# A two-layer block with experts on one core: phase sums with heads on partitions, part of the rounding on GpSimd, the shared expert moved to the logits, and a new order table

## The chip, the cores and the metric

The kernel runs on 1 core of a Trainium2 chip. The metric is the device time of the whole kernel in microseconds (us), taken as the median of three runs. A separate profiled execution gives the trace; its own time is stated beside the runs below.

## The reference, cut to what matters

The input x has 16 sequences of 512 tokens with 128 channels. Four stages follow one another, each with a residual sum and a layernorm:

```python
x = layernorm(x + L0_attn(x))   # 16 heads of 64: cumulative sums along the sequence, with gates
x = layernorm(x + L0_ffn(x))    # 8 experts, one per token (argmax), relu
x = layernorm(x + L1_attn(x))   # 16 heads of 8: softmax attention with a table of position biases
x = layernorm(x + L1_ffn(x))    # one shared expert for all tokens + 8 routed ones (argmax), swiglu
```

Two parts of it are touched by the change. In the first attention, two phases are added to the scores; they depend on the position n and not on the data:

```python
n  = linspace(0, 1, 512)
p1 = sum(sin(a1 * n + b1) * c, axis=-2)      # a1, b1, c: (16 heads, 64, 1) -> (16, 512)
p2 = sum(sin(a2 * n + b2) * c, axis=-2)
```

In the last stage the shared expert is `shared_out = (silu(x @ wg.T) * (x @ wu.T)) @ wd.T`, where x is the output of the third stage's layernorm; the routed experts' output and the residual are added to it. The routing logits are `x @ gate_w.T` of the same x.

## The kernel before

**The program as a list of operations.** The kernel does not issue instructions as it goes through its loops. Each step is handed to a planner with `op(engine, cost, emit, reads, writes)` (L215): an engine, an estimated cost in us, a function that emits the instructions, and the tiles read and written. When all 6210 operations are known, `order()` (L243) fixes one sequence of all of them. It takes, on each engine that its clockwork shows as free, the operation with the lowest rank whose inputs are there and whose buffers can be had. The ranks come from the table `ORDER` (L52): two characters per operation, in the order in which the operations were declared; with DIGITS (91 characters) their place is 91 times the first index plus the second. The places in the table are a permutation, that is a complete order. At the end (L1751 and below) the chain of operations is emitted in this order, so each engine's queue, SP's queue of transfers and GpSimd's queue among them, is fixed when the program is built. An engine works its queue strictly from the front.

**Buffers.** Tiles come from pools by kind (`kinds`, L331): among them six of `w2` (128 x 1024 floats), five of `p`, four of `ld`, three of `mid`, two of `xt` (128 x 512), eight of `x`, which hold the sequences, and in PSUM three of `pair` and two of `one`.

**The head.** `phases` (L471) makes the sines. The 16 x 64 = 1024 sine rows of a phase lie on 128 partitions in 8 groups; a "quarter" is two groups in one `w2` tile `arg`. For each quarter: VectorE makes one angle row (`first`, L478), ScalarE the other (`second`, L484); ScalarE divides by 2 pi and rounds with two activations (`whole`, L491 and L494); VectorE takes whole turns off with two scalar_tensor_tensor instructions and clips (`reduced`, L499 and L502); ScalarE takes the sine (L511). When all four quarters of a phase are there, `sums` (L517 to L524) multiplies on TensorE: for each of 4 token blocks, 8 matmuls with a 128 x 128 block of sines as the stationary operand and `cblk` with 16 columns as the moving one, so that tokens come out on partitions and heads along the free axis. The result is copied to `p1`, or clipped and exponentiated to `p2e`. Many first loads carry `p1` as a gate: the list of tokens to be cleared (`lists`, L693), the experts' table (`table`, L544), `ow`, `wr`, `br` and `rev` are issued on SP behind it. `slide` (L568) builds the position bias: a line per head goes to DRAM, 16 transfers `slid<-line` (L627) bring 128 shifted copies back, and TensorE reverses each (`turn_ps`, L636).

**The two attentions.** `attention0` (L971) computes scores, gates and then four token tiles per sequence (`tile0`, L1038): values `pv` (L1048), their product with the scores `ev` (L1061), GpSimd's product `self` (L1067), the carry of the tile before added by a transfer from GpSimd's queue (L1074), the prefix product `cum` (L1083) and the way out through `po` and `y`. `attention1` (L1210) goes over 4 groups of 4 heads and 4 token tiles: a rounded pass for the maxima (`s`, L1286 and L1293, `low`, `tops`), then scores `st` (L1359), bias sum on VectorE (L1374), exponential on ScalarE (L1380), product `av` (L1389).

**The experts.** Sequences go in chunks of 2, 3, 4, 4, 2 and 1. For each chunk tokens are routed (`route`, L721), scattered to a list in DRAM sorted by expert (`scatter`, L839), fetched four slots of 128 tokens at a time (`slots`, L891), multiplied with the weights of the slot's expert, which GpSimd fetches by index, and gathered back (`gather`, L869). In the last stage, `mixture1` (L1483), the chunk's tokens are scaled and scattered, and then, for each sequence of the chunk, comes the shared expert: the sequence is transposed once more (`transposed`, L682: four TensorE transposes and a ScalarE copy, L687 and L690, tiles `pt_m` and `xt_m`), multiplied with `wgs` and `wus` (L1519), joined by `swiglu`, multiplied with `wds` (L1528), added to x in place (L1536) and stored to `out` (L1543). The slots follow. At the end `out` is read back, the routed part is added, and the last layernorm is applied.

`second` (L1652) runs `attention1`, a layernorm and `logits` (L1595) for each sequence of a chunk. `logits` makes a transposed copy `xt` of the same x.

Of the kernel before, what the change touches and what calls it, by code (L numbers as in the profile page):

```python
# [52 lines left out]
    "###$#P#8#N#R#H#1#6#<#B#Q#.#0#4#>#L#?#3#A#J#W#@#/#F#U#[#_#i#O#9#T#]#a#Y#Z#^#b#c#d#e#h#q#v#g#k#o#u"  # L53
    "#|$$$*$,#)#&#*#l#~$##z#y#n#}#p#I#V#`#G#E#%#,#-#S#(#M#D#X#m#s$/$2$5#w$&$;$+$1$8$@$D$G$I$K#t$-$A$F"
    "$J$N$O$P$X$]$b$e$H$T$Y$^$f$j$k$o$v$z%3%7$_$d$g$m${$~%#%&%*%-%2%8%>%@%E%I%L%O#r#K#'$i$n$p$t$y$|$}"
    "%%%(%)%.%/%0%6%:%<%A%1%4%5%;%B%F%G%J%N%P%R%V%?%C%D%K%U%X%Y%]%`%b%h%k%Q%S%T%Z%c%f%g%j%n%t%z%|&%&)"
    "&,&-&.&0&1&2&8&=&D&U&3&6&;&a&:&l&p&t&y'#')',&b'-&|'$'@'C'F'J'L&r'M'O'T'`'f'j'n'o'''p'q'u(&(+(2(5"
    "(7(=(N(Q(Z(^(O(_(e(l(t#:#2#5#7#;#C#f#j$r%$%'$E$U$Z#{$%$.$)$:$>$B$M$R$L$[$`$a$l$s$3$=$C$S$q$w$'$6"
    "$9$($7$<#x$0$4$?$Q$V$x%H%M$u%9%=$W$c$h&$%v%y#=(a(c(m(y(f(r(u(k(p(x)#(s(w)$).({):)l)o)b)k){)])a)-"
    ")3)m)5);)9)?)I)@)C)0)7)O*)*/*1)+)6)')2)%)8)/)4*J*M*R*Q*U*Y)B)F)D)J)T*o*t*x*s*u*z)H)M)K)P)Z*y*|*~"  # L60
    "*}+$+,)W)^)Q)V)d+#+*+/+&+++2)_)g)U)Y)w)}*#*'+5+9+@)p)q)i)j+'+-+)+(*T*[*_*W*Z*h*L*P*:*A*S*f*i*l*j"
    "*q*v*8*<*4*9*C+0+3+8+6+:+D*+*0)~***6+7+B+H+;+A+L*>*D*%*-*G*`*d+4+Q+V+Z)e)c)X)[+C+>+?+<+G+N+T+S+X"
    "+b)z*&*2*5*;+Y+_+a+`+d+h)u)y)r)v*(+e+k+p+g+m+{*B*F*]*a*e+x+|,$+~,',+)x)|)n)t*,+J+M+O,/,4,7+n+r+v"
    "+q+s,@,(,,,1,0,3,J,5,:,>,F,M,`,E,L,S,R,W,c,f,{-#-7-C-I-R-U-Y-g-j-n.,.4+},%-]-d,.,<,6,;,8,V,T,=,D"
    ",A,C,Q,K,r,w,x,~-(-+-0,a,d-9,p,s,X,_,y,k,o-3-<-D-T-^-a,H,I,?,Y,[,O,N,U-l-p-t-s-w-},v,z,|-'-1-x.#"
    ".+.&.-.0,],b,g,j,m.*.1.6...2.;-$-,---5-?.7.<.C.B.F.R,i,l,n,q,u-G-N-P.W.^.b-2-/-8-;.:.@.?.=.D.H.L"
    ".K.S.c-E-J-~.%.).T.[.a.Y.].h-@-F-X-`-i._.i.m.f.j.y-V-Z-M-S-b.k.s.x.o.t/(-c-h-_-f-m.9.>.J/+/2/8-)"
    "-*-6-4.u.p.q.r.v.z.}.|/$/*-:->-B-H-L/%/)/-/,///5-=-A-Q-W-[/7/;/>/</@/D.'./-u-|.5/A/E/I/H/L/R-o-r"
    "-K-O-y.P.V.~/V/`/c/./1/6/4/9/G/J/N/Q/P/T/[/U/X/Z/Y/b/h/a/g/j/i/m/q/v/x/|00070C0T0`0f0k0v0x0~1&%+"
    "%,%W%[%^%_%a%d%e%i%l%m%q%r%s%x%~&&&+%p%u%{&(&/&4&5&9&>&A&G&L&#&'&*&7&<&?&@&C&J&N&S&W&B&F&O&R&X&["  # L70
    "&^&`&c&i&m&o&s&v'('+'.'1%o%w%}&E&H&I&K&M&Q&P&T&]&V&Y&Z&_&g&j&x&{&d&h&k&q&z&}&~'&'*'/'8'>&n&u&w'%"
    "'4':';'?'B'E'['a'0'3'6'='D'G'H'K'P'W']'b'e'h'w'z'|(#&e&f'2'5'7'9'<'A'I'N'X'U'Y'Z'_'d'i't'x'R'V'^"
    "'c'm'r's'v'y'}(-(3'g'k'l'{(*(.(/(1(6(:(;(@'~(%(((0(9(<(>(A(C(J(U(V(](d(j(o(q(z(})()1)A)L)f*$)&))"
    ")G*=)=*H*K*b*g+R+W+[*?+]+f+i+t+y,9,B,^*N,G,t,}-e-k-q-v-z+l-{.$.(.G.N.X.`.d-%.e.g.l.{/&/:/?/B/O/l"
    "/p/t/z/f0%0*010@/y090G0O0Y151<1A1O1=1@1F1[1C1q1W1_1x2)1{2'20282;2>1H1P2,2:21272@2r2w2x2*1K22252Q"
    "2]2V2Z2a3,33362&323T3V3f4%3k3n404L4P4S264Q5$5(5w695}6&6@787=7B3Y:j6b6i;#;&;';);+;/;3;5;A;`;h;i;m"
    ";s;x;S;j;w;|;~<)<,#+/~0$050=0&0-020.0/06080A030D0Q0J0:0M0V0X0^0d0o0u0w1#1(0_0h0S0Z0s0I0P0[0a0n12"
    "171:0>0U0R0N0H0?0B0K1u1w1z1y2#2%0y1'0q0z1,1}2+2.2$2(2/0c0m0l0p0{24292<2=2A2K1+111)1-1;2B2D2I2H2P"
    "2U0g0j1.191J1S1X1]2Y2c2f0t0r0}0|2F2G2E2J2O2T2^2W2[2p1G1M1D1I1U2e2j2o2i2k2y181>1N1Y1g2l2s2u2q2t3)"
    "141B1?1E1^2v2z3$3#3&311$1*1L1R1b1o1t2S35393?101/16132{2|3%2~3'3*3.3-303O1V1e1`1c1j343;3A383=3U1Q"  # L80
    "1T1l1p1|3H3K3L3R3X3d1d1h1f1k1s3Q3[3_3W3]3j1r1v1Z1a2-2?2b3+3m4#4)3a3g3i3h3p443r3w3}3|4(494/474=45"
    "484A5?5C5I5G5L5T5Y5d5i5l5o5r5y5~6%64676;6?6C3^3e3l3q3o3s3t3y3v4-4*4.3~433z3x3{4O4T4>4E4W4J4M4F4I"
    "4N4m4q4R4V4x4i4n4U4Z4s5,51534$4,4&415F5H5B5D5J5N5P5O5U5p4v4|4_4c5&5V5]5_5^5b6'4D4G4b4g4l5j5u5{5s"
    "5v60464:4<4?4C6#6*6/6.62654H4K4]4`4d595>5Q686A6D4r4p4Y4[6(6,6-6)63666<6:6>6H4}5%4o4u5/6E6I6L6K6O"
    "6Z5'5*4t4w556S6W6]6a6f6j50565-525<6g6v6{6r6x7+575:5m5q5z6U6Y6[70717>4{4z4f4h6o6k6p6m757:7A797;7F"
    "6J6N6_6c6h7<7C7J7@7D7M6|7#6q6u7-7I7K7P7O7T7W6P6T6X6`6e7U7Y7^7]7c7y7/736d6l7H7L7N7Q8#8+827e7k7r7p"
    "7w7}7s8$8*7z8&8-8'8,808.838881858>8;8@8C8G8K8N8O8W8`8h8m8r8y9+9/929F7X7[7_7f7a7l7n7j7g7m7o7~7q8%"
    "7u7x7t8R8e8A8D8i8=8J8M8T8^8V8Z8?8B8d8E8P848:8U8n8s8w7{7|8)8(8789868<9-969A91989E90938p8v9:9C9G9L"
    "9J9P9V8H8L8c8g8q9K9O9R9Q9U9_8j8z8[8a9#9S9]9d9b9f9j9&9*8l8o9.9H9I9M9p9t9v8Y8]8S8Q9Y9[9a9W9e9h9m9k"
    "9y9~8}9'9)9,9>9z9}:&:#:-:9979;999=9B:0:8:=:5:;:@9<9@9g9i9n:>:G:J:B:H:V9l9q9o9s9x9|:%:':[:`:e9594"  # L90
    "8x8u:C:F:D:A:X:_:f:Z:b:r:$:)9r9w:,:g:l:n:m:q:w:(:+:.:1:<:o:u:z:s:v;,:6:?:I:M:Q:y:|:~:};%;8:O:S:L"
    ":P:U:Y:^:a;=;L;O;2;:;?;7;<;N;>;C;E;D;H;P;F;K;R;Q;U;X;V;Z;_;];c;e;g;k;n;p;r;u;}<%<*<-</<0<1<2'S'Q"
    "($('()(,(4(8(?(B(G(H(L(M(P(R(S(W([(D(I(K(Y(b(g(h(n(v(~)N)S(T(X(`(i(|),)*)<*E*I*O*X*.*3*7*@*V*^*c"
    "*k*m+o+u+w+z,&,e,h-&-.(F(E)>)E)R)`)h)s*r*w*{+=+E+F+K+P+U,P,Z+%+.+1+I,#,*,),2.3.8.n.w+^+c+j,-.M.Z"
    ".Q.U/0/3/e/o/=/C/F/K/k/s/w0#0'0;0E0L0W0]0b0e0i1%*p*n.A.E.I.O/#/'/M/S/]/W/^/_/d/n/r/{0)0,040<0F1i"
    "1m1n232X2_2h2n/u/}0+1~2C2M2N2R373:3B3I2`2d2g2m2}3(3/3>3F3u4'4+424;4@4B4e4k0(2L3<3@3E3G3M3P3J3N3S"
    "3Z3b3`3c5)5.5A5K4X4^4a4j4y4~5#5+5;5@5[5c54585=5E5`5e5f5n5t5x5|6$5M5S5X5h6+616=6B6F6M6Q6R6V6^6n6s"
    "6t6y6z6~7'72777R7h8/7%7(7d8F7E8X8_8f8k8t8|9$8I9%8{8~9?9D9N9T9^8b9X9Z9`9u9{:*:/:29(:3:4:7:R:W:c:h"
    ":k9c;4:t:x;J;M;T;W;Y::;a;[;b;q;v;{<#<&<.<B<E<I<P<?<R<V<c<n<X<r<z=g=n='=H>(>->2<3<4<8<=<5<6<9<O<<"
    "<j<7=L<><A<C<G<H<J<N<a<k<o<K<M<Q<S<U<Z<]<i<x<~<:<;<@<L<D<F<T<Y<_<`=j=<=w=}>/>=>6>9>B>F>J>N=i>K>I"  # L100
    ">M>y?6?#?.?;?R?Y?Z>$?X?L?OB#C$B)B/C+C4C;C=>QC:CGCQC}DlD'D*DtESEYE]?SI2F.F9IJIMIOIQIRITI[I_IgJ4J;"
    "JCJKJPJTJ>NwO%O-O7OCOML&O)O?ONOQOlOp<W<[<q<w<^<g<e<b<d<l<y<f<h=0=/=2<m=B=F=8=A=K=1=7<v<}=?=-=4=$"
    "=+=9=U=X<|=&=u>'>.>1=#=*<u<s<{=%=,<t>V>[>_>^>b>e=E=I=J=O=[>`>d>g>f>j>o=G=M=6=:=R>t>z>}>w>{?-=W=_"
    "=N=T=d>~?%?+?*?/?3=]=b=@=C=k=q=x={?7?:?>=Z=Y=>==?'?&?,?)?0?5?9?8?<?A=m=p=z>#>,???B?G?E?I?N=t=y>+"
# [101 lines left out]
class Plan:  # L206
# [8 lines left out]
    def op(self, engine, cost, emit, reads=(), writes=(), delay=None):  # L215
        if delay is None:
            delay = (0.25, 0.12, 0.15, 0.15, 3.4)[engine]
# [104 lines left out]
def block_kernel(ctx: ExitStack, tc: tile.TileContext, d, out: bass.AP):  # L322
# [144 lines left out]
    def col(t):  # L467
        return slice(t * P, (t + 1) * P)
# [1390 lines left out]
```

## Time and profile before

| what | us |
|---|---|
| median of 3 runs | 2387.21 |
| lowest and highest run | 2380.75, 2396.14 |
| profiled execution, its own time | 2306.71 |
| span of the profile (first to last instruction) | 2305.0 |
| TensorE busy in the span | 2123.2 |
| VectorE busy | 1805.3 |
| ScalarE busy | 1468.9 |
| GpSimd busy | 759.6 |

The profile is of one execution, which was shorter than the three timed runs. Lines of the profile name the engine (PE is TensorE's matmuls, PEld its weight loads, DVE VectorE, ACT ScalarE, POOL GpSimd, SPq the issuing of transfers on SyncE), the source line, the operation and the tiles, written as output<-input with buffer numbers left out. A group has "busy, mean ns of one" and, behind the next bar, the idle time of the engine just ahead of it and what ended it. One fp32 matmul of the program shows as two records on PE. Times of a timeline are in us from the span's start: start, length, and for the engine that waited, in brackets, how long and for what.

### The profile page before, as it was taken

Reading aid. Unit: us, or ns where it says so; the run is one execution under the profiler, and the core shown is the slowest. Engines: PE = TensorE matmul, PEld = TensorE weight load, DVE = VectorE, ACT = ScalarE, POOL = GpSimd, SP = SyncE. Lnnn points to the kernel's source line nnn. Section 1 sums busy time; section 2 is a strip of 40 time slices with the busy share of each in tenths; the row PEclk is TensorE's granted clock in tenths of the full one; section 3 lists DMA queues with packets and bytes.
Section 4 is the critical chain, followed back from the end, with each engine's and each line's share of the span. In section 5 each row is a group of like instructions: output and inputs, shape, how many; then the busy total and the mean of one; then the engine's idle time right before and its main releaser. Section 6 shows DMA issues by size and latency. Waiting matters only on the chain. (4 is left out here: it accounts for less than half of the span.)

```text
span 2305.0 us, 34824 instructions
## 1 busy us (share of the span) xinstructions
PE 2123.2 (92%) x12723; PEld 1086.2 (47%) x12820; DVE 1805.3 (78%) x3286; ACT 1468.9 (64%) x1848; POOL 759.6 (33%) x763
## 2 busy tenths in 40 slices
PE   5898989999999998999999998999999999998994
PEld 4465744444545445454443443455534334544353
DVE  6355698788879787888878687988887999687973
ACT  6322367866576784667567876557687876676651
POOL 1134552134121425621214234422231424223524
PEclk9898999999999998999999998999999999999997
DMA  6522321211210333320102331212232211432334
GB/s 178 158 91 71 92 70 42 69 45 49 77 45 11 85 111 93 97 87 10 41 14 67 105 105 28 74 52 79 73 86 71 68 38 56 135 116 74 111 106 145
DMA packets 152446, 180.03 MB, mean 78 GB/s; under 512 B 19332, under 2 KB 125444, under 8 KB 152276
## 3 DMA queue, kind: packets, MB, share of 16 engines
q1 hardware_dynamic: 125588, 84.27, 13.7%
q0 software_dynamic: 26688, 93.53, 13.7%
q8 instruction: 101, 1.65, 0.3%
q14 instruction: 69, 0.57, 0.1%
HBM read 127.67 MB, written 42.93 MB: 74 GB/s over the span
## 5 line engine op out<-in xcount | busy, mean ns | idle before, releaser
L1380 ACT ACTIVATE p<-p 128x1024 f32<-128x1024 f32 x512 | 537.4, 1058 | 237.1 <-DVE p L1374 222.3
L1374 DVE TENSOR_TENSOR p<-st,bias 128x1024 f32<-128x1024 f32 x512 | 604.3, 1217 | 90.4 <-PE st L1359 80.3
L1308 ACT CAST low<-s 128x1024 bf16<-128x1024 f32 x512 | 495.0, 1020 | 113.6 <-PE s L1293 91.1
L823 POOL DMA_INDIRECT ws<-tab,rows x212 | 215.7, 1017 | 460.4 <-PE py L962 168.0
L1316 DVE TENSOR_TENSOR low<-low 128x1024 bf16<-128x1024 bf16 (+1 forms) x512 | 299.5, 585 | 78.7 <-ACT low L1308 69.8
L1359 PE MATMUL st<-qk_pad 32*128 32x512 f32 x2048 | 319.5, 646 | 3.9 <-DVE p L1374 3.6
L1286 PE MATMUL s<-bias,ident 128*128 128x512 bf16 x927 | 301.6, 398 | 10.3 <-ACT low L1308 3.2
L1389 PE MATMUL av<-p,vaug 128*32 128x512 f32 x2048 | 282.3, 609 | 7.6 <-ACT p L1380 6.2
L1067 POOL TENSOR_TENSOR self<-ev,own 128x1024 f32<-128x1024 f32 x64 | 125.3, 1957 | 429.1 <-DVE ev L1061 309.6
L1293 PE MATMUL s<-qk_pad 32*128 32x512 bf16 x1024 | 204.2, 391 | 24.0 <-issue 14.7
L1317 DVE TENSOR_REDUCE tops<-low 128x4 f32<-128x512 bf16 x256 | 175.5, 686 | 10.4
L1293 PEld LDWEIGHTS <-qk_pad 32*128 32x128 bf16 x1024 | 48.9, 91 | 244.0 <-issue 227.5
L823 POOL DMA_INDIRECT yg<-results,place x128 | 128.3, 1002 | 95.3 <-issue 38.3
L1359 PEld LDWEIGHTS st<-qk_pad 32*128 32x128 f32 x2048 | 93.6, 184 | 128.6 <-DVE p L1374 44.8
L1286 PEld LDWEIGHTS <-ident 128*128 128x128 bf16 x1024 | 75.1, 100 | 145.8 <-issue 142.7
L1083 PE MATMUL cum<-ev,tri 128*128 128x512 f32 x256 | 132.0, 640 | 10.5 <-DMA ev<-carry 8.6
L1114 PEld LDWEIGHTS y<-ow,ot 128*128 128x128 f32 x1024 | 122.7, 194 | 32.1 <-issue 19.2
L1114 PE MATMUL y<-ow,ot 128*128 128x128 f32 x1024 | 130.0, 281 | 2.1 <-DVE cnt L808 1.3
L1048 PE MATMUL pv<-vw,xt 128*128 128x512 f32 x256 | 128.1, 625 | 0.0
L962 PE MATMUL py<-ws,h 128*128 128x128 f32 x848 | 111.2, 285 | 9.3 <-DVE h L1478 5.2
L1061 DVE TENSOR_TENSOR ev<-pv,ex 128x1024 f32<-128x1024 f32 x64 | 78.0, 1219 | 52.8 <-PE pv L1048 25.9
L962 PEld LDWEIGHTS py<-ws,h 128*128 128x128 f32 x848 | 102.1, 196 | 36.7 <-issue 14.5
(191 smaller groups left out, 2903.4 us busy)
## 6 DMA issues: line engine op xcount, KB each, us to landing
xq<-tokens SPq DMA_DIRECT2D x44, 256.0 KB
results<-yq SPq DMA_DIRECT2D x44, 256.0 KB
qk_pad<-qk SPq DMA_DIRECT2D x256, 32.0 KB
slid<-line SPq DMA_DIRECT2D x16, 448.0 KB
tokens<-zero SPq DMA_DIRECT2D x4, 1472.0 KB
x<-in_x SPq DMA_DIRECT2D x16, 256.0 KB
xt<-in_xt SPq DMA_DIRECT2D x16, 256.0 KB
qk_pad<-qk SPq DMA_DIRECT2D x256, 16.0 KB
```

Source lines behind the costliest of these rows:

```text
L823: nc.gpsimd.indirect_dma_start(out, bass.IndirectOffsetOnAxis(to, 0) if to is not None else None, in_, bass.IndirectOffsetOnAxis(of, 0) if ...
L962: nc.tensor.matmul(py()[:, col(s)], h()[:, c, col(s)], ws[s]()[:, off + c * W : off + (c + 1) * W], start=(c == 0), stop=(c == 1),)
L1114: nc.tensor.matmul(y()[:, :P], ot()[:, hf, col(c)], ow[:, 4 * hf + c, :], start=(hf == 0 and c == 0), stop=(hf == 1 and c == 3),)
L1286: nc.tensor.matmul(s()[:, i, :], ident16, bias16[:, 4 * g + 2 * jp + i, 2 * u + 1 : 2 * (u + N) : 2], start=True, stop=False,)
L1293: nc.tensor.matmul(s()[:, i, :], pad[r, 0, col(it)], pad[r, 1, :], start=False, stop=True,)
L1308: lambda s=s, jp=jp, part=part: nc.scalar.copy(part(0, N)[:, 2 * jp : 2 * jp + 2, :], s()),
L1316: nc.vector.tensor_tensor(part(0, n), part(0, n), part(n, 2 * n), ALU.max)
L1317: nc.vector.tensor_reduce(tops[g % 2][:, it, :], part(0, N // 4), AX.X, ALU.max, negate=True)
L1359: nc.tensor.matmul(s[jp]()[:, i, :], pad[r, 1, col(jt)], pad[r, 0, :], start=True, stop=True,)
L1374: lambda jp=jp, h=h, pj=pj: nc.vector.tensor_tensor(pj(), s[jp](), bias[:, h : h + 2, u : u + N], ALU.add),
L1380: ACT, 1.0, lambda pj=pj: nc.scalar.activation(pj(), pj(), AF.Exp),
L1389: nc.tensor.matmul(acc()[32 * j : 32 * j + 32, :], va[:, jt, h * VW : h * VW + 32], p[j // 2]()[:, j % 2, :], start=(jt == 0), stop=(jt == ...
```

## The change

- **Phases.** Each quarter's sines are now the moving operand and `cblk` (16 columns) the stationary one: two matmuls of 512 columns per quarter, as soon as that quarter is done, accumulate heads on 16 partitions. ScalarE copies the sum (in a `us` tile), and four transposes bring tokens back on partitions.
- **Rounding.** In the odd quarters `whole` becomes two tensor_scalar instructions on GpSimd; in the even ones it stays on ScalarE.
- **Shared expert.** A new function `shared` holds what stood in `mixture1`. It is called in `second` right behind `logits`, for each sequence, and uses the transposed copy that `logits` made; the extra transposition goes. Its sum goes to a new `mid` tile `kept`, not to x, and is stored from there.
- **Costs.** The planner's default hand-over delays and some of its costs are changed (a stretch of such edits that hold no other change is left out below: `pv` and `cum` 1.72 to 1.8, `low` 1.03 to 0.93 and the like).
- **Order table.** All of `ORDER` is new. It has 6188 places in place of 6210 (10 operations more in the phases, 32 fewer in the transpositions), again a permutation. Read out, SP's queue begins with `lin`, `ab` and the clearing of two token lists; four `slid` transfers (heads 14, 13, 0, 15) stand ahead of the clearing of a third list and of the experts' table, the fifth (head 9) behind them; on TensorE the turns of these five heads stand ahead of the first `cum`, that of head 9 ahead of the gates' sums; VectorE copies `p1` behind the last `reduced`; the loading of `kone` comes later. In the last chunk the shared expert's first matmul stands ahead of `rank`.

```diff
 ORDER = (
-    "###$#P#8#N#R#H#1#6#<#B#Q#.#0#4#>#L#?#3#A#J#W#@#/#F#U#[#_#i#O#9#T#]#a#Y#Z#^#b#c#d#e#h#q#v#g#k#o#u"
...
+    "###$#J#>#9#F#;#'#)#,#2#=#*#-#/#<#M#1#0#6#H#S#P#(#Q#b#g#K#U#^#m#q#w#z#4#+#C#Z#a#A#.#D#T#]#_#h#k#o"
...
 )
@@ -214,7 +213,7 @@
 
     def op(self, engine, cost, emit, reads=(), writes=(), delay=None):
         if delay is None:
-            delay = (0.25, 0.12, 0.15, 0.15, 3.4)[engine]
+            delay = (0.13, 0.11, 0.12, 0.1, 3.4)[engine]
         o = Op(len(self.ops), self.due, engine, cost, delay, emit)
         self.ops.append(o)
         before = set()
@@ -505,26 +504,43 @@
 
                 op(ACT, 0.6, second, reads=["ab", lin], writes=[(arg, 1)])
                 op(DVE, 0.53, first, reads=["ab", lin], writes=[(arg, 0)])
-                op(ACT, 1.9, whole, reads=[(arg, 0), (arg, 1)], writes=[turns])
+                def whole_too(arg=arg, turns=turns):
+                    nc.gpsimd.tensor_scalar(turns(), arg(), INV2PI, ROUND, ALU.mult, ALU.add)
+                    nc.gpsimd.tensor_scalar(turns(), turns(), ROUND, None, ALU.subtract)
+
+                if quarter % 2:
+                    op(POOL, 4.0, whole_too, reads=[(arg, 0), (arg, 1)], writes=[turns])
+                else:
+                    op(ACT, 2.3, whole, reads=[(arg, 0), (arg, 1)], writes=[turns])
                 op(DVE, 3.2, reduced, reads=[turns], writes=[arg])
                 op(
-                    ACT, 1.0, lambda arg=arg: nc.scalar.activation(arg(), arg(), AF.Sin),
+                    ACT, 1.1, lambda arg=arg: nc.scalar.activation(arg(), arg(), AF.Sin),
                     writes=[arg],
                 )
                 sines.append(arg)
-            acc = buf("one", f"phase{which}")
-
-            def sums(acc=acc, sines=sines):
+            acc, sums = buf("one", f"phase{which}"), buf("us", f"sums{which}")
+            for quarter, sines_of in enumerate(sines):
+
+                def add(acc=acc, arg=sines_of, quarter=quarter):
+                    for j in (2 * quarter, 2 * quarter + 1):
+                        nc.tensor.matmul(
+                            acc()[:H0], cblk[:, j, :], arg()[:, j % 2, :], start=(j == 0),
+                            stop=(j == 7),
+                        )
+
+                op(PE, 3.0, add, reads=[sines_of, "cblk"], writes=[acc])
+            op(
+                ACT, 0.6, lambda acc=acc, sums=sums: nc.scalar.copy(sums()[:H0], acc()[:H0]),
+                reads=[acc], writes=[sums],
+            )
+
+            def turn(acc=acc, sums=sums):
                 for t in range(NT):
-                    for j in range(8):
-                        nc.tensor.matmul(
-                            acc()[:, t * H0 : (t + 1) * H0],
-                            sines[j // 2]()[:, j % 2, t * P : (t + 1) * P],
-                            cblk[:, j, :],
-                            start=(j == 0), stop=(j == 7),
-                        )
-
-            op(PE, 8.0, sums, reads=[*sines, "cblk"], writes=[acc])
+                    nc.tensor.transpose(
+                        acc()[:, t * H0 : (t + 1) * H0], sums()[:H0, col(t)], ident[:H0, :H0]
+                    )
+
+            op(PE, 0.6, turn, reads=[sums], writes=[acc])
 
             def av(acc=acc):
                 return acc()[:, : NT * H0].rearrange("p (t h) -> p t h", h=H0)
@@ -659,7 +675,7 @@
             for t in range(NT):
                 nc.vector.bn_aggr(mv()[:, t, :], st()[:, t, :])
 
-        op(DVE, 1.3, stats, reads=[x, *xs_of(x)], writes=[st, mv])
+        op(DVE, 1.08, stats, reads=[x, *xs_of(x)], writes=[st, mv])
 
         def scale():
             nc.gpsimd.tensor_scalar(rs(), mv()[:, :, 1], EPS, None, ALU.add)
...
@@ -1480,6 +1496,41 @@
         )
         return h
 
+    def shared(b, x, xt):
+
+
+        pg, pu = buf("pair", f"pg_s{b}"), buf("pair", f"pu_s{b}")
+        for w, ph, key in ((wg, pg, "wgs"), (wu, pu, "wus")):
+
+            def up(w=w, ph=ph):
+                for f in range(2):
+                    nc.tensor.matmul(ph()[:, f, :], w[:, col(f)], xt(), start=True, stop=True)
+
+            op(PE, 1.82, up, reads=[xt, key], writes=[ph])
+        h = swiglu(pg, pu, NT, f"s{b}")
+        py, kept = buf("one", f"py_s{b}"), buf("mid", f"kept_{b}")
+
+        def products():
+            for t in range(NT):
+                for f in range(2):
+                    nc.tensor.matmul(
+                        py()[:, col(t)], h()[:, f, col(t)], wd[:, f, :],
+                        start=(f == 0), stop=(f == 1),
+                    )
+
+        op(PE, 1.89, products, reads=[h, "wds"], writes=[py])
+        op(
+            DVE, 0.65,
+            lambda: nc.vector.scalar_tensor_tensor(
+                kept(), py(), 0.5, x(), ALU.mult, ALU.add
+            ),
+            reads=[py, x, *xs_of(x)], writes=[kept],
+        )
+        op(
+            SP, 0.45, lambda: nc.sync.dma_start(xout[b], tok(kept())), reads=[kept],
+            writes=[("out", b)],
+        )
+
     def mixture1(c, b0, xs, lg, store, span):
         n = f"m1_{c}"
         nt = CHUNKS[c] * NT
@@ -1508,42 +1559,6 @@
                 reads=[x, m], writes=[scaled, ("scaled", c, i)],
             )
             scatter(1, c, i, scaled, place, store)
-        for i, x in enumerate(xs):
-            plan.due = span(0.1 + 0.2 * i / len(xs))
-            xt = transposed(x, f"{n}_{i}", [("scaled", c, i)])
-            pg, pu = buf("pair", f"pg_{n}_{i}"), buf("pair", f"pu_{n}_{i}")
-            for w, ph, key in ((wg, pg, "wg"), (wu, pu, "wu")):
-
-                def up(w=w, ph=ph, xt=xt):
-                    for f in range(2):
-                        nc.tensor.matmul(ph()[:, f, :], w[:, col(f)], xt(), start=True, stop=True)
-
-                op(PE, 1.82, up, reads=[xt, key + "s"], writes=[ph])
-            h = swiglu(pg, pu, NT, f"{n}_{i}")
-            py = buf("one", f"pys_{n}_{i}")
-
-            def products(py=py, h=h):
-                for t in range(NT):
-                    for f in range(2):
-                        nc.tensor.matmul(
-                            py()[:, col(t)], h()[:, f, col(t)], wd[:, f, :],
-                            start=(f == 0), stop=(f == 1),
-                        )
-
-            op(PE, 1.89, products, reads=[h, "wds"], writes=[py])
-            op(
-                DVE, 0.65,
-                lambda x=x, py=py: nc.vector.scalar_tensor_tensor(
-                    x(), py(), 0.5, x(), ALU.mult, ALU.add
-                ),
-                reads=[py], writes=[x, *xs_of(x)],
-            )
-
-            op(
-                SP, 0.45, lambda i=i, x=x: nc.sync.dma_start(xout[b0 + i], tok(x())),
-                reads=[x], writes=[("out", b0 + i)],
-            )
-
         def expert(k, xqt, ws, yq, n, done):
             pg, pu = buf("pair", f"pg_{n}"), buf("pair", f"pu_{n}")
             for off, ph in ((0, pg), (F1, pu)):
@@ -1615,6 +1630,7 @@
                 nc.vector.tensor_copy(to, lgv)
 
         op(DVE, 0.2, store, reads=[lg, "br"], writes=[dst, (dst, i)])
+        return xt
 
     def inputs(b):
         xt, x = buf("ld", f"xt0_{b}"), buf("x", f"x_{b}")
@@ -1654,7 +1670,7 @@
             at = float(ROUNDS * (b0 + i))
             attention1(b0 + i, x, at)
             layernorm(x, f"2_{b0 + i}")
-            logits(x, gw, "gw", lg, i, f"l1_{b0 + i}")
+            shared(b0 + i, x, logits(x, gw, "gw", lg, i, f"l1_{b0 + i}"))
 
```

## The prediction

> **What bounds the kernel now.** I read the page's busy shares first, then the engines' busy time in four stretches, then the timeline of the first 70 us, then the groups by shape and TensorE's waits.
>
> ```profile
> span 2305.0 us, 34824 instructions
> PE 2123.2 (92%) x12723; PEld 1086.2 (47%) x12820; DVE 1805.3 (78%) x3286; ACT 1468.9 (64%) x1848; POOL 759.6 (33%) x763
> ```
>
> TensorE is the bound as a whole. By stretch (columns: length, busy of PE, PEld, DVE, ACT, POOL, clock, DMA share, GB/s):
>
> ```profile
> 0.00:70.00 70.00, 40.58 (x157) 32.21 (x158) 36.87 (x44) 39.85 (x41) 7.79 (x39) 0.86 0.73 191
> 70.00:130.00 60.00, 54.75 (x228) 33.07 (x227) 25.16 (x46) 22.68 (x25) 16.05 (x11) 0.96 0.60 185
> 130.00:2230.00 2100.00, 1988.25 (x12095) 986.01 (x12191) 1715.28 (x3108) 1395.46 (x1766) 700.68 (x675) 0.98 0.25 69
> 2230.00:2305.00 75.00, 39.66 (x250) 34.87 (x248) 27.98 (x88) 10.96 (x17) 35.12 (x39) 0.79 0.45 138
> ```
>
> Of 182 us in which TensorE is idle, 29 lie in the head, 5 after it, 112 in the 2100 us of the middle (95% busy) and 35 in the tail. So three things can pay: less TensorE work in the middle, a shorter head, smaller gaps.
>
> **The head.** Its timeline, cut to what sets the pace:
>
> ```profile
> 27.12 13.80 PE L520 MATMUL phase<-cblk,arg 128*128 128x16 f32 x64
> 38.40 0.55 DVE L478 TENSOR_SCALAR arg<-lin,ab 128x512 f32<-128x512 f32 x1 [4.26 <-PE phase L520]
> 40.96 0.23 DVE L534 COPY p<-phase 128x64 f32<-128x64 f32 x1 [0.49 <-PE phase L520]
> 45.97 9.08 SPq L627 DMA_DIRECT2D slid<-line  x1
> 48.81 0.69 DVE L502 TENSOR_SCALAR arg<-arg 128x1024 f32<-128x1024 f32 x1
> 50.65 10.93 PE L520 MATMUL phase<-cblk,arg 128*128 128x16 f32 x52 [0.57 <-ACT arg L511]
> 61.61 0.23 DVE L462 TENSOR_SCALAR p2e<-phase 128x64 f32<-128x64 f32 x1 [1.27 <-PE phase L520]
> 66.84 3.33 PE L636 MATMUL turn_ps<-slid,flip 128*128 128x448 f32 x4 [5.27 <-DMA slid<-line]
> 69.96 2.67 PE L1083 MATMUL cum<-ev,tri 128*128 128x512 f32 x4
> ```
>
> The sums hold all `w2` buffers until 38.4, so the last quarters of phase 2 start late; its sums end at 61.6. But the first prefix product, at 70, waits for a bias row whose transfer is late (66.84).
>
> **Part 1, sums with heads on partitions.** Before: 64 records per phase, 0.215 us each (13.80/64), all after the last sine. After: 8 matmuls of 512 columns, 16 records per phase, two matmuls (4 records) as soon as a quarter is done. A 512-column record is in the trace at 0.86 and, later in the same burst, at 0.43 us (eight `pv` records from 40.76 took 5.40). Here a rule weighs: the Trainium skill's page "TensorE: Matmul & The Clock Gate", Part 1, says that the array runs at half rate until it has been busy for a window of about 3.4 us. The clock column reads 1.00 up to 50 us and 0.55 from 50 to 60, though thin records take the same 0.21 us in both (10.93/52), so here I go by durations. The 64 thin products never left 0.215 in 13.8 us, while `pv` changed pace after some 3.6: so the wide form can warm the clock, but spread by quarters it may not. The last quarter costs 1.7 us warm, 3.4 cold; I take 3.4. Then the copy out (0.59, row `us<-av`), four transposes (8 records at 0.12 to 0.25, I take 1.0). From the last clip to `p2e`, before: 61.61 - 49.50 = 12.1 us. After: sine 1.05 + 3.4 + 0.6 + 1.0 + 0.35 for hand-overs = 6.4. Gain 5.7 behind the last clip.
>
> **Part 2, rounding on GpSimd.** Four of eight roundings (1.13 + 1.15 us each) leave ScalarE: 9.1 us off it. They become eight `tensor_scalar` of 128x1024 on GpSimd. No row shows that one; a memset of that size takes 0.94, the two-input product `self` 1.90. I take 1.2, since it reads one tensor. A rule speaks against the change: "SBUF — State Buffer", section "SBUF: two separate sides", says that GpSimd and a VectorE instruction with two SBUF inputs, or in a two-port mode, exclude each other for the whole instruction. This trace agrees:
>
> ```profile
> 1844.87 3.00 DVE L1201 SCALAR_TENSOR_TENSOR x<-yg,m,x 128x128 f32<-128x128 f32 x4
> 1845.01 1.92 POOL L1067 TENSOR_TENSOR self<-ev,own 128x1024 f32<-128x1024 f32 x1
> 1861.33 1.13 DVE L1201 SCALAR_TENSOR_TENSOR x<-yg,m,x 128x128 f32<-128x128 f32 x4
> ```
>
> Four such steps take 1.13 alone and 3.00 beside `self`: longer by 1.87, all of the GpSimd instruction. The reductions beside the rounding (L499) are of that kind. So VectorE's chain carries both. Its sum: first reduction at about 10 (first angle at 7.8, slowed by the memsets, then 2.3 of rounding); eight reductions of 2 x 1.22 + 0.69 = 3.17 make 25.4; two late angles 1.1; small copies of the order table 2.0: 38.6 without exclusion, 48.2 with it (8 x 1.2), 54.3 with 1.96. Before: 49.5. So the last clip moves by -11 to +5; I take -1. `p2e` then comes at 48.2 + 6.4 = 54.6, 7 us sooner.
>
> **What is late next.** The new table puts `p1` behind the last reduction on VectorE: about 48.5, where it was 40.96. Behind `p1` on SP's queue stand the clearing of a token list (1.47 MB), the expert table (2.5 MB, without its small parts) and only then the fifth bias row; on TensorE that row's turn stands ahead of the first prefix product. At about 250 GB/s (the 50 to 70 us slices show 252 and 258) that is 18 us: 66.5, as before. What is gained is that four bias rows (4 x 1.67 us of TensorE) and the gates come ahead of this wait instead of behind it, in time that stood empty. Head: -6 us; ends -14 (no exclusion: `p1` at 39) and +4 (1.96 per rounding: the row lands at 72). The clearing of two lists at the very front of SP delays `cblk` to about 18; six `w2` buffers let the angles go on, so it costs nothing; with fewer it would cost those 4 us.
>
> **Part 3, shared expert beside the logits.**
>
> ```profile
> L687 PE MATMUL pt_m<-ident,x 128*128 128x128 f32 x64 | 12.0, 319 | 1.0 <-ACT xt_m L690 1.0
> L690 ACT COPY xt_m<-pt_m 128x512 f32<-128x512 f32 x16 | 9.5, 594 | 10.8 <-PE pt_m L687 9.9 <-PE pu_m L1519 0.7
> L1316 DVE TENSOR_TENSOR low<-low 128x1024 bf16<-128x1024 bf16 x256 | 182.8, 714 | 69.9 <-ACT low L1308 69.8
> ```
>
> The transposes go: 12.0 us of TensorE, at 95% busy worth 11. The rest (33.1 + 30.6 + 32.1 us of TensorE, two VectorE products and one sum, one store per sequence) only moves. It moves from behind each chunk's routing to the end of each sequence. The store then stands earlier on SP, ahead of the next group's small copies, and waits for the sum, about 1 us behind the product: no cost while those copies lead by more than that. `kept` takes one of three `mid` buffers for some 3 us, 16 times: nothing, unless an expert's tile wants it then. In the tail the new table has one shared matmul ahead of `rank`, 1.7 us against the choosing's 1.2: +0.5 at most.
>
> **Part 4, the order.** The table gives every operation its place; read out, its head and tail are as told above. In the middle the distance in TensorE operations from `pv` to `cum` grows from 16.2 to 19.3, from scores to `av` stays at 6.5, from `cum` to `po` falls from 14.0 to 12.9. TensorE's waits that it bears on:
>
> ```profile
> PE po L1106 <- DVE o L1099: 12.0, 7, 5.1
> PE s L1293 <- DMA qk_pad<-qk: 9.3, 12, 2.3
> PE cum L1083 <- DMA ev<-carry: 8.6, 5, 2.8
> PE av L1389 <- ACT p L1380: 6.2, 8, 1.7
> ```
>
> None is large, so no order can give much: of 112 us in the middle I take a tenth, -10. Ends: -45 (the four rows and as much again from the many small ones) and +35 (1 us more in each 58 us slice).
>
> **Sum.** 2306.7 for the profiled execution - 6 - 11 - 10 = 2280, a ratio of 0.988. The timed median is 2387.2, 80.5 us above the profiled execution, for which the trace has no row; I carry the ratio over: 2359 us.
>
> **Rivals.** (a) The order closes twice what it should: -45 in place of -10: 2245 profiled, 2323 timed. For: 112 us of gaps; against: they are many and short. (b) Nothing comes of it: the exclusion costs what ScalarE saves, the expert table lands later (+4), the order is neutral or takes back half of the transposes: about -2, 2385. For: the late `p1`. (c) Slower: cover lost at the chunk changes. An attention step loads VectorE with 2 x 1.22 + 0.71 + 0.46 + 0.69 = 4.3 us and TensorE with (319.5 + 282.3 + 301.6 + 204.2)/256 = 4.3: no slack. The shared work, 95.8 us rich in TensorE, stood there as filling while routing and scatters ran. If each of the five changes opens 10 us, +50 - 17 - 10 = +23: 2411 timed. It decides from 27/5 = 5.4 us per change. Against: 870 to 928, a change, already idles 9 us with that filling in reach.
>
> **Chances.** Likeliest case 0.50, its own range 2335 to 2378, two thirds of it under 2363; (a) 0.16; (b) 0.22; (c) 0.12. Measurement tells about 1% from no change (three runs spread by 0.65%). Faster by over 1%: 0.34 + 0.16 = 0.50, and a little of (b): 0.52. Slower: (c) beyond 2411 and near it, 0.11. Same: 0.37. Range for 8 in 10: 2320 (a) to 2408, which leaves out most of (c).
>
> **What would show it.** Right: no `pt_m` or `xt_m`; phase records of 512 columns; `p2e` at 50 to 58; L499 longer than 1.22 beside GpSimd; TensorE busy near 2110 less what the clock gives; first `cum` near 70 with five bias turns ahead of it. Wrong: `p2e` before 48 (no exclusion); `p1` late with TensorE idle past 75; gaps over 5 us where a chunk is routed; middle gaps off 112 by more than 30.

## The result and the profile after

| | median, us | runs |
|---|---|---|
| before, in the same comparison | 2383.98 | 2370.05 to 2396.14, 4 runs |
| changed kernel | 2348.5 | 2342.62 to 2362.61, 4 runs |
| ratio | 0.9855 | 95% interval 0.9812 to 0.9898 |

The profile of before that the prediction rests on was an uncommonly quick execution (2306.7 us, below every timed run), so the trace after is set beside a second profile of before, span 2396.4, called "before again" (its run is the first experiment).

The page of the changed kernel, its span and busy shares:

```profile
span 2342.1 us, 34607 instructions
PE 2148.8 (92%) x12668; PEld 1055.8 (45%) x12668; DVE 1809.5 (77%) x3286; ACT 1452.9 (62%) x1824; POOL 782.2 (33%) x771
```

TensorE is idle for 193.3 us, where before again has 2396.4 - 2156.1 = 240.3 and the first profile of before 181.8. It is busy for 2148.8 us, against 2156.1 and 2123.2, though 12 us of transposes are gone. Two executions of the unchanged program thus lie further apart than the change moves either number, so these totals do not show whether the gain is gaps closed or work removed.

Part of what sets the two profiles of before apart are pauses of ScalarE and VectorE that end with a signal for which the profile shows no sender (the view calls it "remote"). The first profile has none longer than 1.5 us; before again has ten, 64 us in sum. The longest holds ScalarE for 20.9 us (up to 986.5), and TensorE waits behind it:

```profile
PE sc L977 <- ACT vaug L1224: 16.9, 1, 16.9
```

The changed kernel's profile has five such pauses, 20 us in sum, and every profile of the experiments has some. What causes them is open.

By stretch (columns as before: length, busy of PE, PEld, DVE, ACT, POOL, clock, DMA share, GB/s):

```profile
0.00:70.00 70.00, 33.28 (x76) 9.22 (x76) 43.94 (x48) 32.47 (x36) 25.90 (x47) 0.87 0.75 182
60.00:70.00 10.00, 0.00 (x0) 0.00 (x0) 0.00 (x0) 0.00 (x0) 0.00 (x0) 0.58 1.11 192
70.00:130.00 60.00, 51.27 (x192) 29.85 (x193) 22.77 (x33) 18.98 (x21) 13.87 (x9) 0.90 0.67 199
130.00:2267.00 2137.00, 2030.19 (x12196) 987.04 (x12195) 1718.72 (x3134) 1392.93 (x1755) 711.60 (x682) 0.97 0.24 68
2267.00:2342.00 75.00, 34.04 (x206) 29.65 (x204) 24.02 (x72) 8.56 (x13) 30.84 (x34) 0.73 0.42 128
```

The middle holds 107 us of TensorE idle in 2137 us, the first profile of before 112 in 2100, before again 164 in 2191. The head did not get better: from 60 to 70 us all five engines stand still, and the transfers alone are busy. The head's timeline after, cut as it was for before (start, length, then what was waited for):

```profile
18.48 1.24 POOL L508 TENSOR_SCALAR turns<-arg 128x1024 f32<-128x1024 f32 x1 [4.10 <-ACT arg L483]
18.73 4.03 DVE L498 SCALAR_TENSOR_TENSOR arg<-turns,arg 128x1024 f32<-128x1024 f32 x2
19.80 3.62 POOL L509 TENSOR_SCALAR turns<-turns 128x1024 f32<-128x1024 f32 x1
32.22 2.47 DVE L498 SCALAR_TENSOR_TENSOR arg<-turns,arg 128x1024 f32<-128x1024 f32 x2
44.44 0.69 DVE L501 TENSOR_SCALAR arg<-arg 128x1024 f32<-128x1024 f32 x1
45.05 0.22 DVE L550 COPY p<-phase 128x64 f32<-128x64 f32 x1
46.91 1.89 PE L526 MATMUL phase<-arg,cblk 128*16 128x512 f32 x4
50.95 0.22 DVE L461 TENSOR_SCALAR p2e<-phase 128x64 f32<-128x64 f32 x1 [3.23 <-PE phase L539]
72.41 3.16 PE L652 MATMUL turn_ps<-slid,flip 128*128 128x448 f32 x4 [14.92 <-DMA slid<-line]
75.40 0.33 PE L1015 MATMUL ce<-ex,tri 128*128 128x64 f32 x2
76.21 1.75 PE L652 MATMUL turn_ps<-slid,flip 128*128 128x448 f32 x4
77.80 1.88 PE L1099 MATMUL cum<-ev,tri 128*128 128x512 f32 x4
```

`p2e` is ready at 51 in place of 61.6, but the fifth bias row's turn waits 14.92 us for its transfer, and the first `cum` begins at 77.8, later than before's 70. Only three of the four earlier rows are turned by then: the gates' sums (`ce`), whose input was ready at 48.1, and the fourth of those rows stand behind the waiting turn in TensorE's queue. The first routing (`rank`) is at 178.0, against 179.6 and 177.5 in the two profiles of before: the head gives nothing.

SP's queue shows what the row waited for:

```profile
44.19 0.43 SPq L723 DMA_DIRECT2D tokens<-zero  x1
44.66 5.81 SPq L578 DMA_DIRECT2D tab<-in_b  x1
65.12 0.84 SPq L643 DMA_DIRECT2D slid<-line  x2
```

The clearing of the third list is issued at 44.19, before `p1` is copied at 45.05. So the gate `p1` fixes a place in the planner's order, but SP does not wait for `p1` on the chip. The row's lateness comes from what SP has ahead of it, however early `p1` is.

TensorE's waits that answer to those shown of before:

```profile
PE po L1122 <- DVE o L1115: 5.8, 8, 1.8
PE s L1309 <- DMA qk_pad<-qk: 13.9, 7, 3.8
PE cum L1099 <- DMA ev<-carry: 5.4, 2, 4.6
PE av L1405 <- ACT p L1396: 9.6, 11, 1.8
```

Against the first profile none of them grew or fell by more than 7 us; against before again, `s` waits 10 us longer here (13.9 for 3.7). No row of this view shows where the gain lies.

### The profile page after: what moved, and what is told of

Its sections match the earlier page's. It is cut to its first block, busy times and chain, and to the rows that moved or that the text cites. A ratio compares the mean times of both kernels' runs of the same rounds, so it can differ in the third digit from the quotient of the medians.

```text
span 2342.1 us, 34607 instructions
## 1 busy us (share of the span) xinstructions
PE 2148.8 (92%) x12668; PEld 1055.8 (45%) x12668; DVE 1809.5 (77%) x3286; ACT 1452.9 (62%) x1824; POOL 782.2 (33%) x771
## 4 chain that ended last, share of the span: by engine, by line
PE 62%; DVE 19%; issue 5%; ACT 5%; DMA 3%; POOL 3%; SPq 2%; another core or an unknown queue 1%; POOLq 0%; DVEq 0%; ACTq 0%
PE st L1375 9%; PE s L1302 8%; PE av L1405 8%; PE s L1309 5%; DVE p L1390 4%; PE pv L1064 4%; PE py L978 4%; PE y L1130 3%; DVE low L1332 3%; PE cum L1099 3%; PE po L1122 2%; PE ph L1182 2%; PE pg L1569 2%; DVE tops L1333 2%; DVE o L1111 1%
## 5 line engine op out<-in xcount | busy, mean ns | idle before, releaser
L1332 DVE TENSOR_TENSOR low<-low 128x1024 bf16<-128x1024 bf16 (+1 forms) x512 | 294.8, 576 | 112.8 <-ACT low L1324 91.1
L1302 PE MATMUL s<-bias,ident 128*128 128x512 bf16 x1024 | 336.5, 411 | 23.0 <-ACT low L1324 10.9
L1309 PE MATMUL s<-qk_pad 32*128 32x512 bf16 x1024 | 210.6, 405 | 14.1 <-DMA qk_pad<-qk 13.9
L1064 PE MATMUL pv<-vw,xt 128*128 128x512 f32 x256 | 133.3, 646 | 0.9 <-DVE o L1111 0.6
L681 POOL TENSOR_SCALAR rs<-mv 128x4 f32<-128x4 f32 x64 | 22.9, 358 | 316.2 <-DVE mv L676 315.3
L1111 DVE TENSOR_TENSOR o<-cum,gg 128x1024 f32<-128x1024 f32 x64 | 78.1, 1220 | 50.3 <-PE cum L1099 31.2
```

The lines of the kernel that those rows point to most:

```text
L1064: nc.tensor.matmul(pv()[:, hf, :], xt()[:, col(t)], vw[:, hf * N : (hf + 1) * N], start=True, stop=True,)
L1302: nc.tensor.matmul(s()[:, i, :], ident16, bias16[:, 4 * g + 2 * jp + i, 2 * u + 1 : 2 * (u + N) : 2], start=True, stop=False,)
L1309: nc.tensor.matmul(s()[:, i, :], pad[r, 0, col(it)], pad[r, 1, :], start=False, stop=True,)
L1332: nc.vector.tensor_tensor(part(0, n), part(0, n), part(n, 2 * n), ALU.max)
```

## The experiments

My theory after the result: the middle is set by how well the written order fits the work, and that is worth far more than the 10 us I gave it; the removed transposes and the new head are worth little. The rivals: the removed work makes the gain ("work"); or moving the shared expert costs cover at the chunk changes, whatever the order ("cover"). In all experiments but the first, `order()` reads the table and nothing else, so that the table alone fixes every queue. Ratios are to before in the same comparison; the rounds ran on different chips (before took 2404.62, 2388.57 and 2405.64 us), so across rounds the ratios are compared and not the times. "Searched" tables came from moving operations a few places at a time and keeping what shortens the kernel's own clockwork over the changed kernel's costs.

**1. Before again.** No edit.

> The kernel before, unchanged. The profiled execution shown of it took 2306.7 us, its timed runs 2370 to 2396; the profile of the changed kernel is one of its own timed runs (2343.8). Theory A (the short profiled execution was an exception, the same program at a better moment of the chip): a new profile spans about 2375 us, with the same gaps but longer middle stretches. Theory B (profiling itself shortens this kernel): again near 2305.

2398.15 us in one run, clock 0.946; before in this comparison 2404.62. Theory B is out, since this profiled execution is as long as the timed ones. The quick profile was an exception, as theory A says, with the clock at 0.966. But the new one is 21 us longer than the 2375 expected, and the gaps are not the same: 240.3 us of TensorE idle in place of 181.8.

**2. Only the shared expert moved.**

```diff
+            shared(b0 + i, x, logits(x, gw, "gw", lg, i, f"l1_{b0 + i}"))
...
-        for i, x in enumerate(xs):
...
-            xt = transposed(x, f"{n}_{i}", [("scaled", c, i)])
...
```

Phases and rounding are those of before; all other operations keep before's order, and the shared ones stand as far behind `lg` as in the changed kernel.

> Only the shared expert's move (part 3); phases, rounding and all other places of the order as before, the moved operations put behind the logits at the distances that the new table has. Prediction's step: 12.0 us of TensorE transposes go, worth 11 us, ratio 0.995. Rival 'the move itself pays' (even load along a sequence): 30 us or more, ratio below 0.988. Rival 'cover lost at the chunk changes': 10 us per change, ratio above 1.01.

1.0274, interval 1.0233 to 1.0314: less work, and 2.7% slower. Where? I cut the span at the copies of the second layer's logits, one for each sequence. The steps in which a chunk ends and the next begins show it; the second, third and fourth of the five, first in before again:

```profile
939.00:1165.00 226.00, 198.32 (x1074) 96.33 (x1084) 171.15 (x315) 126.61 (x147) 70.75 (x66) 0.90 0.19 53
1489.00:1710.00 221.00, 214.66 (x1314) 115.23 (x1327) 185.49 (x306) 133.43 (x153) 69.80 (x65) 0.98 0.25 72
1972.00:2128.00 156.00, 142.96 (x911) 75.75 (x918) 114.67 (x204) 99.21 (x131) 50.27 (x52) 0.97 0.35 101
```

the same steps with the shared expert moved and nothing else:

```profile
964.00:1178.00 214.00, 182.84 (x1018) 86.41 (x1030) 164.94 (x310) 122.72 (x142) 70.60 (x66) 0.93 0.20 53
1520.00:1743.00 223.00, 204.33 (x1219) 106.51 (x1231) 175.17 (x296) 127.66 (x146) 69.54 (x65) 0.93 0.24 68
2041.00:2200.00 159.00, 135.86 (x823) 70.10 (x823) 105.46 (x194) 93.65 (x123) 49.98 (x52) 0.91 0.32 94
```

and in the changed kernel:

```profile
924.00:1120.00 196.00, 184.59 (x985) 86.98 (x985) 157.54 (x288) 113.81 (x131) 68.37 (x61) 0.93 0.20 55
1449.00:1606.00 157.00, 150.11 (x856) 72.62 (x854) 142.29 (x275) 96.53 (x110) 63.82 (x60) 0.98 0.21 60
1937.00:2036.00 99.00, 93.01 (x627) 46.21 (x626) 84.00 (x164) 72.46 (x86) 40.04 (x40) 1.00 0.33 96
```

Length less PE busy is TensorE's idle time. In the second step shown the chunk's four shared experts are gone from behind the routing (TensorE busy 10 us less), yet the step is no shorter: the idle time went from 6.3 to 18.7; in the third from 13.0 to 23.1. Over all five changes it went from 72.4 to 104.8, or 6.5 us more at each; over the ten other steps from 59.8 to 71.9. In each of the two profiles one wait of the first step shown stands behind a pause without a sender (16.9 us in before again, 12.3 here); without them it is 55.5 and 92.5. The first profile of before has only 39.8 us at its five changes, so the loss is real in its direction and uncertain in its size. That is the prediction's rival (c) at work. The changed kernel has 44.6 us at the five changes, between before's two profiles. Its second and third step are 64 and 57 us shorter than before again's, 10 and 7 of it the work that left them in experiment 2, while the step behind the second is longer (125 us against 61): I read this as the next chunk's first stage being spread among the attentions of the second, where before did more of it in one piece.

**3. All of the changed work, the old order.** The changed kernel's operations and its head; from the routing of the second chunk on, before's order with the shared operations put in as in 2.

> All the new work (phases, rounding, shared expert) with the new table's head, but from the third sequence's first product on the order of before. Measured so far: after/before 0.9855, 35 us. Prediction's steps: without the new middle order -17 us, ratio 0.993, leaving 10 us or a little more to the order. Rival 'the order carries it' (head about nothing, transposes 11): ratio 0.994 to 0.996. Rival 'the move of the shared work carries it': ratio 0.987, as the changed kernel.

1.0263, interval 1.023 to 1.0297. None of the three expectations comes near. The same operations as the changed kernel's, 4.1% apart: the order alone makes some 97 us.

**4. The shared expert put back, the new order.** The changed kernel with `mixture1`'s loop and its transposes back behind the routing.

> The changed kernel with the shared expert put back behind each chunk's routing, with its own transposes; new head, new order elsewhere. Prediction's steps: -16 us, ratio 0.993. Rival 'the order carries it': about -24 us, ratio 0.990. Rival 'the move carries it': ratio 0.998 or more.

1.0237, interval 1.0204 to 1.027. Again none of the expectations comes near: with this work back behind the routing, the new table is as bad as the old one for the moved work.

**5. Only the new head.** Before with the new phases, rounding and head's order; from the routing of the second chunk on, before's order.

> The kernel before with the new phase sums, the rounding on GpSimd and the new order of the head only; from the routing of the second chunk on, every operation stands where it stood before, and the shared expert is not moved. The prediction gave the head -6 us: a ratio of 0.9975. The two traces after the fact put the first routing only 1.6 us sooner: 0.999. Theory 'a mixture of two orders costs some two per cent by itself' gives over 1.015; if it comes out at 0.995 to 1.003, a mixed order is not slow for being mixed.

1.0023, interval 1.0001 to 1.0045: 5.5 us slower by the ratio, 2.4 by the medians. The first routing stands at 183.1 us, 5.6 later than in before again. So the head gives nothing when the old order follows, and a mixture of two orders need not be slow: this is one and costs 0.2%.

**6. Only the order.** Before with nothing changed but the table, searched. A row of it:

```diff
 ORDER = (
...
-    ")3)m)5);)9)?)I)@)C)0)7)O*)*/*1)+)6)')2)%)8)/)4*J*M*R*Q*U*Y)B)F)D)J)T*o*t*x*s*u*z)H)M)K)P)Z*y*|*~"
+    ")C)M)8)<)n)t)y);)>)=)A)G*1*6*9)5)*(x)/)6)1)')7*F*P*U*O*R*^)Z)`)P)U)i*m*s*v*t*y*z)^)e)N)R)o*x*{*~"
...
 )
```

> The kernel before with nothing changed but its order table from the routing of the second chunk on: the same operations, searched anew for places in which each engine's queue finds its inputs ready. Theory 'order' (what the change gained is the fit of the order to the work, not the removed transposes) expects 0.980 to 0.992, most of the gain of the whole change. Theory 'work' (the gain is the transposes and the head; an order can give little, as the prediction's term of -10 us says) expects 0.995 to 1.003.

0.9926, interval 0.99 to 0.9951: 18 us for a table, just above what I expected of theory "order", below what "work" allows, and half of what the whole change gained. The table also swapped two pairs of VectorE steps and the place of five early loads in the head; the first routing came 5.5 us sooner (172.0 against 177.5), so about 12 of the 18 us lie in the middle.

**7. The shared expert alone moved, with a searched order.** Kernel 2 with another table.

> The kernel e1_shared_alone (only the shared expert moved beside the logits, no transposes of its own, measured 1.027) with its order searched anew from the routing of the second chunk on, the head as before. Theory 'order': the 1.027 was the places of the moved operations and of those around them, so it falls to 0.985 to 0.998. Theory 'cover' (the prediction's rival c: the shared work is missing as filling at the chunk changes, wherever it stands now) keeps it at 1.010 or over.

1.0041, interval 1.002 to 1.0062, between the two expectations. Of the 2.7% of kernel 2 the order gave back 2.3; some 8 us of it lie ahead of the first routing (173.1 against 180.8). TensorE's idle time over its five chunk changes is 68.3 us, no longer 104.8: the lost cover can be replaced. It did not reach before itself: this search, which begins at before's table, did not find what the changed kernel's table has.

**8. The changed kernel, searched further.** Another table from the second chunk's routing on.

> The changed kernel with its order table searched further from the routing of the second chunk on, head as it is. The changed kernel itself is at 0.9855. Theory 'order' expects a little more from the same means: 0.974 to 0.984, with less TensorE idle between 130 us and the tail than its 107 us. Theory 'work' expects 0.983 to 0.990, no further gain.

0.9822, interval 0.9785 to 0.9858: within "order", but its interval reaches into "work" and overlaps the changed kernel's, so it does not decide. Its profiled run, one of the longer ones, has 117 us of TensorE idle in the middle, not below 107: that part of the expectation missed.

**9. The head's transfers in another order.** SP's queue behind the first four bias rows, in the changed kernel and here:

```diff
-zeros0_0 ld_tab0_3 ld_br ld_tab0_1 ld_tab0_2 ld_tab0_0 ld_wr slid9 slid5 ld_rev ld_ow slid4 slid6 slid2 slid1 slid7 ...
+slid9 slid5 ld_ow slid4 slid6 zeros0_0 slid2 slid1 ld_tab0_3 slid7 slid11 ld_tab0_1 slid3 slid12 ld_tab0_0 slid8 ...
```

> The changed kernel with nine transfers of the head put elsewhere on SP's queue: the clearing of the third list goes behind the seventh bias row, the four parts of the experts' table, ow, wr, br and rev go between or behind the next bias rows, so the fifth row stands directly behind the four. Theory 'queue' (the fifth row was late because 4 MB of clearing and table stand ahead of it): its turn starts at 55 to 62 us instead of 72.4, the wait of 14.9 us in front of it falls below 5, and the ratio falls by 0.003 to 0.006 against the changed kernel's 0.9855, to 0.979 to 0.983. Rival 'bandwidth' (the transfers share the same engines, so what is put behind is only late elsewhere): the turn comes sooner, but the first routing stays at 178 us and the ratio at 0.985.

0.9794, interval 0.976 to 0.9829. TensorE here:

```profile
55.24 3.17 PE L652 MATMUL turn_ps<-slid,flip 128*128 128x448 f32 x8
59.05 1.75 PE L652 MATMUL turn_ps<-slid,flip 128*128 128x448 f32 x4
60.64 1.88 PE L1099 MATMUL cum<-ev,tri 128*128 128x512 f32 x4
```

The fourth and fifth turn run on without a wait, the first `cum` stands at 60.6 in place of 77.8, the first routing at 162.5 in place of 178.0. Those 15.5 us are 0.0065 of 2400; the ratio fell by 0.0061 against the changed kernel's of another round. In its own round it is 12 us below kernel 10, whose row is as late as the changed kernel's (2355.6 against 2367.46). Theory "queue" holds: the head's end was set by what SP had ahead of one row, and "bandwidth" is out, since the first routing came sooner although the clearing and the experts' table had to wait.

**10. All rounding on ScalarE.**

```diff
-                if quarter % 2:
+                if False:
                     op(POOL, 4.0, whole_too, reads=[(arg, 0), (arg, 1)], writes=[turns])
```

> The changed kernel with all eight roundings on ScalarE; GpSimd rounds nothing, all else as it is. Theory 'exclusion' (GpSimd's rounding and VectorE's reductions hold each other up, so it gives nothing): the last clip ends at 43 to 49 us (45.1 in the changed kernel), every L498 takes 1.2 to 1.3 us, ratio within 0.002 of the changed kernel's. Rival 'ScalarE sets the pace' (the 9.1 us are saved on the path): last clip at 52 or later, p1 and the fifth bias row as much later, ratio 0.003 higher.

0.985, interval 0.9817 to 0.9884: the same as the changed kernel. The reductions' group in this kernel (busy, mean ns of one):

```profile
L498 DVE SCALAR_TENSOR_TENSOR arg<-turns,arg 128x1024 f32<-128x1024 f32 x16 | 19.6, 1222 | 8.0 <-ACT turns L493 7.8
```

Each takes 1.22 us again, but VectorE waits 7.8 us for ScalarE's rounding; `p1` comes at 46.4 against 45.1, `p2e` at 53.6 against 51.0, and the fifth row's turn at 72.3 against 72.4. GpSimd's half gains 1.4 to 2.6 us on the chain, all of it lost in the wait for the row. All signs of theory "exclusion" came. SP issues the clearing at 40.77 here, 5.6 us ahead of `p1`, and the row comes no later: again nothing on SP waits for `p1`.

**11. The shared expert put back, with a searched order.** Kernel 4 with another table.

> The kernel e1_shared_back (new head, the shared expert put back behind the routing with its own transposes, measured 1.024) with its order searched anew from the routing of the second chunk on. Theory 'order': the 1.024 was places again, so it falls to 0.985 to 0.997, and what is left between it and the changed kernel with a searched order (0.982) is what the move itself is worth: the 12 us of transposes make 0.005. Rival 'work' (the move itself makes the gain): it stays at 1.000 or over.

0.985, interval 0.9812 to 0.9889: as much as the whole gain of the change, with the shared expert where it was and every transpose still there. Set against kernel 8, which has the move and a searched order (how far each search went is not on record), the move is worth a ratio of 0.9822/0.985 = 0.997; with the two intervals put together (half widths 0.0037 and 0.0039) 0.992 to 1.003. "Work" falls: the gain can be had without the move. A small worth of the move is neither shown nor ruled out.

**12. Both together.** The changed kernel with 9's queue and a table searched further than 8's.

> Two steps together on the changed kernel: the head's transfers as in e3_slid_first and the order from the routing of the second chunk on searched further than in e2_after_fit (0.982). If both gains stand side by side: 0.974 to 0.980, faster than both kernels. If the sooner start of the first attention is waited away at the first routing: 0.980 to 0.984.

0.9706, interval 0.9664 to 0.9749, 2331.73 us where before had 2405.64: better than expected, and faster than both kernels.

## Why the prediction was right, and where its steps were not

The sum was -27 us on 2306.7, a ratio of 0.988; measured was 0.9855. That the sum came out near is luck: two of its three terms were off, in opposite directions, and the third is not resolved.

**The head, predicted -6 us: nothing.** The steps up to `p2e` were right and even on the cautious side. From the last clip to `p2e`: 5.8 us for 6.4; the last quarter's matmuls took 1.89 us, the warm value, where I took 3.4. The last clip ended at 45.1 and not at 48.2, since the exclusion fell mostly on the other engine: 16 reductions took 23.3 us, 3.7 more than the 19.6 of before, where I had put 9.6 (two clips took 0.5 us more each), while the four second roundings on GpSimd took 12.8 us in place of four times some 1.2. The step that failed is "what is late next": 18 us from `p1` to the landing of the fifth row. The row does not hang on `p1` at all, and from the clearing's issue to the row's turn it took 28.2 us (44.19 to 72.41). I reckoned 4 MB and the row at 250 GB/s; the trace has 218 GB/s in this stretch, some 6.1 MB. By 44.19 only some 0.7 of the four earlier rows' 1.8 MB can have passed (168 GB/s from 39.78), and a further row was issued beside the fifth. So bytes that I left out make most of the miss and the lower rate the rest.

**The transposes, predicted -11 us: not resolved.** `pt_m` and `xt_m` are gone as said. Experiments 8 and 11 put the whole move at -7 us, with -20 to +6 open. -11 lies within; nothing shows it.

**The order, predicted -10 us with ends -45 and +35: the term that was mis-sized.** On before's own work a search gave 18 us, some 12 of them in the middle; on the new head with all old work (experiment 11) 2405.64 - 2367.35 = 38 us (36 by the ratio), with a first routing no sooner than before's (181.1 us). So the order is worth 18 to 38 us where I put 10, and at the upper end rival (a) had the better size for it. My reason for a small gain was that no wait is large. That was the wrong reading: 38 us over 256 attention steps are 0.15 us a step, far below any wait that the view lists by itself; and two tables on the same work lie 97 us apart.

**Rival (c), cover lost at the chunk changes.** The mechanism is real: in experiment 2 it cost 6.5 us a change against before again and 13 against the first profile, above the 5.4 from which I said it decides. But it is a property of the old order with the work taken out, not of the move: under the new table the idle time there is 44.6 us, where before has 39.8 and 72.4.

**Chances.** The likeliest case came by its class and near its time, but by terms that made up for each other: the head gave 6 us less than forecast, the order 8 to 28 more. Of the signs named, the first `cum` near 70 failed (77.8); the middle's gaps stayed near 112, which I now know to vary by 50 us between two executions of before.

What stays open: the tables were compared as wholes, and which of some thousand moves matter was not tried. The pauses without a sender have no known cause, and how much of each timed run they make is not known either. Busy time of TensorE rises though the work is less (2185 us in experiment 2, 2149 after, 2123 and 2156 in before's two profiles). Times the mean granted clock it lies between 2022 and 2056 in all fourteen profiles, so a difference in busy time can't be read as work without the clock. The Trainium skill's page "TensorE: Matmul & The Clock Gate", Part 1, section "HAM oscillation — how this bites in real kernels", says that gaps of more than 3.4 us send the array back to half rate. Rows of the changed kernel agree that a wait is paid for twice, but show it from a shorter wait on:

```profile
113.67 3.75 PE L1099 MATMUL cum<-ev,tri 128*128 128x512 f32 x4 [4.56 <-DMA ev<-carry]
123.41 1.88 PE L1099 MATMUL cum<-ev,tri 128*128 128x512 f32 x4
126.85 1.95 PE L1130 MATMUL y<-ow,ot 128*128 128x128 f32 x16
183.98 3.30 PE L1130 MATMUL y<-ow,ot 128*128 128x128 f32 x16 [2.82 <-DVE ex L1002]
```

Behind waits of 4.56 and 2.82 us the next group takes 1.9 and 1.4 us longer than the same group elsewhere; behind one of 1.72 us, in experiment 9, `cum` takes 1.96, about as without a wait. Whether fewer such waits, a higher clock (0.953 after, 0.946 in before again) or both make the gain of an order is open.

## What to carry to other kernels

Where the order of all queues is written out, moving work is half a change: measure it with the order made anew on both sides, since the old table made a lighter program 2.7% slower and a new one made the unlightened program, with a new head that gives nothing by itself, 1.5% faster. Judge an order by its waits added up over a stage, not by the largest, and profile one kernel twice first: two executions of before differed by 58 us of TensorE idle. When a path gets shorter, follow the transfer that ends it to the front of its queue, and look in the trace whether a gate of the plan is a wait on the chip: putting nine transfers elsewhere gave 12 to 15 us, which the whole rebuilt head had not.

## What the runs showed of the hardware

- A `tensor_scalar` of 128x1024 floats on GpSimd takes 1.18 us when nothing holds it up (1.24 to 1.48 in other places) and 2.77 to 3.62 beside VectorE's two-input reductions, which then take 3.24 to 4.03 for two in place of 2.48 (in one of the four places still 2.48). Two clips of one input took 1.17 in place of 0.69 there. Neither engine had plain priority; in these four places GpSimd lost more (8 us against 4.7).
- A 512-column fp32 matmul with only 16 stationary columns takes 0.86 us per record at first and 0.47 in the later bursts of four, about as one with 128 columns does (0.86 and 0.43 before).
- With transfers alone at work (60 to 70 us) 192 GB/s passed; between 40 and 50 us, with four engines busy and other transfers, 262.
- Engines can stand still for up to 20.9 us on a signal without a visible sender: ten pauses, 64 us, in one profile of before, none over 1.5 us in the other.
- SP issues a transfer ahead of a step that only the plan puts before it: the clearing at 40.77 with `p1` copied at 46.41 (experiment 10).
